# Ten held tiles instead of eight, a new block order and a first tile in four chunks in the quantized feed-forward of a gated Flamingo block

## The chip, the cores and the metric

The kernel runs on one core of one Trainium2 chip. The metric is device time in microseconds (us) for one execution of the whole kernel. The core has five engines with queues of their own: TensorE (PE, with its weight loads listed as PEld), VectorE (DVE), ScalarE (ACT), GpSimd (POOL) and SyncE (SP). Nearly all DMAs of this kernel are issued from SP's queue, which takes them strictly in the order in which they stand in it.

## The reference, cut to what matters

```
x = x + tanh(g_xattn) * cross_attention(layernorm(x), ctx)      # 4096 rows of 512
# feed-forward on n = layernorm(x), 512 -> 2048 -> 512
s_x = max|n| / 127 ;  xq = round(n / s_x)                       # one scale for the whole tensor
s_w = max|w| / 127 ;  wq = round(w / s_w)                       # the same for w1 and w2
h   = gelu((xq @ w1q.T + b1) * (s_w1 * s_x))                    # 4096 x 2048
s_h = max|h| / 127 ;  hq = round(h / s_h)                       # max over ALL of h
o   = (hq @ w2q.T + b2) * (s_w2 * s_h)
out = x + tanh(g_ffn) * o
```

The point that shapes the second half is `s_h`: the largest magnitude of all the middle activations `h` must be known before the first of them can be quantized. So no second-layer matmul can start until the whole first layer is done, and all 32 MB of `h` (float32) must be kept somewhere in the meantime.

## The kernel before, in words

The 4096 rows are cut into `NB` = 8 blocks of `TB` = 512 rows, and a block into `NT` = 4 row tiles of 128. Attention runs first (0 to about 440 us) and is not touched by the change; during it the weights are loaded and quantized into `w1q` (a tile of [128, 4, 2048] bf16, 16 KB per partition) and `w2q`. The rows of `x` stay in SBUF as `X[i]` throughout.

**First layer.** Its PE order is written out by hand (blocks 0 to 7, in each 16 feature chunks `fc`, in each 4 matmuls over `KC`). Block 0's quantized, transposed input is `xqT0`, made by PE transposes (L522 to L526). The inputs of the other blocks are made by `quantize_x(i+1)` on DVE: four normalizations of 512 columns (L169), one multiply-and-add-MAGIC over 2048 columns (L184), one subtract over 2048 columns (L185), and four DMA transposes from SP (L561) into `xqT`. The pool `fwork` has two buffers for `xs`, `xq` and `xqT`. Each group of four feature chunks forms one tile `G` ([128, 4, 512] float32, 8 KB per partition), written by four Gelu activations on ACT (L588), reduced for the maximum on DVE two chunks at a time (L598). A block has `GT` = 4 such tiles, so there are 32. The pool `gpool` has `HELD` = 8 buffers: the last 8 tiles (blocks 6 and 7) stay in SBUF in the dictionary `held`, the first 24 are stored to DRAM (L609, tensor `h`), 1 MB each, and come back later.

**The joint.** `scale_of(hmax, ...)` on DVE and PE turns the maxima into `s_h` and `inv_h` (L154 to L164). Then DVE computes `s2` = s_h * s_w2 * tanh(g_ffn) (L612, L613) and scales the bias row `b2_sb` by it (L614).

**Second layer.** Blocks are taken in the order 6, 7, 0, 1, 2, 3, 4, 5: the held ones first. Rounding a tile takes ACT (L634: times `inv_h`, plus MAGIC, in place) and then DVE (L635: minus MAGIC, into the bf16 tile `hq`). Tile 0 of block 6 is special: its first chunk is rounded on DVE alone (L631), its other three by ACT and DVE. The first block in the order runs feature chunks outside and row tiles inside, so that PE can begin with one chunk; every other block runs row tile by row tile, 16 matmuls each (L643), into the PSUM tile `pf` (pool `ps_o`, 4 buffers). Per row tile, POOL adds the bias row to `X` (L657), DVE adds the scaled PSUM result (L661), and SP stores 256 KB of output (L663). Loads of stored tiles, `Gb` (L628), go into `gpool` buffers as these come free. A scheduler places the loads between the output stores in SP's queue and the roundings between the L661 additions in DVE's queue; both queues keep their order at run time.

Of the kernel before, what the change touches and what calls it, by code (L numbers as in the profile page):

```python
# [8 lines left out]
F32 = mybir.dt.float32  # L9
BF16 = mybir.dt.bfloat16  # L10
AF = mybir.ActivationFunctionType
ALU = mybir.AluOpType
# [3 lines left out]
P = 128  # L16
D = 512
KC = D // P
# [9 lines left out]
TB = 512  # L28
NT = TB // P
FF = 2048  # L30
FC = FF // P
GF = 4
GT = FC // GF
HELD = 8
EPS = 1e-5
QP = 127.0
MIN_RANGE = 1e-6
MAGIC = 1.5 * 2.0**23
# [4 lines left out]
def tile_flamingo_gated_block(  # L43
# [20 lines left out]
    nc = tc.nc  # L64
    B = ctxT.shape[0]
    NB = x.shape[0] // TB
    NBB = NB // B

    const = ctx.enter_context(tc.tile_pool(name="const", bufs=1))
# [16 lines left out]
        return w.rearrange("(kc p) n -> p kc n", p=P)  # L86


    actx = ExitStack()
    awts = actx.enter_context(tc.tile_pool(name="awts", bufs=1))  # L90
    wq_sb = awts.tile([P, KC, D], F32, name="wq_sb")
    wo_sb = awts.tile([P, KC, D], F32, name="wo_sb")
# [7 lines left out]
    tg = const.tile([P, 2], F32, name="tg")  # L100
# [26 lines left out]
    mhalf = const.tile([P, NT], F32, name="mhalf")  # L127
    nc.gpsimd.memset(mhalf, -0.5)

    w1q = const.tile([P, KC, FF], BF16, name="w1q")  # L130
    xqT0 = const.tile([P, KC, TB], BF16, name="xqT0")
    w2q = const.tile([P, FC, D], BF16, name="w2q")
    mean2 = const.tile([P, NB, NT, 2], F32, name="mean2")
# [16 lines left out]
    def scale_of(maxima, name, psum, tag):  # L150


        m = const.tile([P, 1], F32, name=f"m_{name}")
        nc.vector.tensor_reduce(m, maxima, AX.X, ALU.max)  # L154
        diag = small.tile([P, P], F32, tag="diag", name=f"diag_{name}", bufs=1)
        nc.vector.tensor_scalar(diag, ident, m, None, ALU.mult)
        pg = psum.tile([P, 512], F32, tag=tag, name=f"pg_{name}")
        nc.tensor.matmul(pg[:, :P], ones, diag, start=True, stop=True)
        g = const.tile([P, 1], F32, name=f"g_{name}")
        nc.vector.tensor_reduce(g, pg[:, :P], AX.X, ALU.max)  # L160
        s = const.tile([P, 1], F32, name=f"s_{name}")
        nc.vector.tensor_scalar(s, g, MIN_RANGE, 1.0 / QP, ALU.max, ALU.mult)
        inv = const.tile([P, 1], F32, name=f"inv_{name}")
        nc.vector.reciprocal(inv, s)  # L164
        return s, inv

    def normalize2(dst, i, t):

        nc.vector.tensor_scalar(  # L169
            dst,  # L170
            X[i][:, t, :],
            mean2[:, i, t, 0:1],
            rstd2[:, i, t : t + 1],
            ALU.subtract,
            ALU.mult,
        )
# [5 lines left out]
    def quantize(dst, src, inv):  # L182

        nc.vector.tensor_scalar(src, src, inv, MAGIC, ALU.mult, ALU.add)  # L184
        return nc.vector.tensor_scalar(dst, src, MAGIC, None, ALU.subtract).ins  # L185
# [5 lines left out]
    with actx:  # L191
# [245 lines left out]
        for i in range(NB):  # L437
            for s in range(2 * NG):
                if s + 2 < 2 * NG:
                    last = softmax(i, s + 2)  # L440
                elif i + 1 < NB:
                    last = softmax(i + 1, s + 2 - 2 * NG)
# [47 lines left out]
                t = s - NT if i == 0 else s // 2  # L490
# [41 lines left out]
        tc.tile_pool(name="hidden_dram", bufs=1, space=bass.MemoryType.DRAM)  # L532
    )

    late = ctx.enter_context(tc.tile_pool(name="late", bufs=1, reuse_waits="tile"))
    b2_sb = late.tile([P, D], F32, name="b2_sb")
    nc.sync.dma_start(b2_sb, b2.to_broadcast([P, D]))

# [7 lines left out]
    with ExitStack() as fctx:  # L546
        fwork = fctx.enter_context(tc.tile_pool(name="fwork", bufs=2, reuse_waits="tile"))
        ps_h = fctx.enter_context(
            tc.tile_pool(name="ps_h", bufs=4, space=PSUM, reuse_waits="tile")
        )  # L550

        def quantize_x(i):

            xs = fwork.tile([P, NT, D], F32, tag="xs", name=f"xs{i}")
            xq = fwork.tile([P, NT, D], BF16, tag="xq", name=f"xq{i}")
            xqT = fwork.tile([P, KC, TB], BF16, tag="xqT", name=f"xqT{i}")
            for t in range(NT):
                normalize2(xs[:, t, :], i, t)
            quantize(xq, xs, inv_x)
            for t in range(NT):  # L560
                nc.sync.dma_start_transpose(xqT[:, :, t * P : (t + 1) * P], xq[:, t, :])  # L561
            return xqT

        s1 = const.tile([P, 1], F32, name="s1")
        nc.vector.tensor_tensor(s1, s_x, s_w1, ALU.mult)
        b1s = const.tile([P, FC], F32, name="b1s")
        nc.vector.tensor_scalar(b1s, b1_sb, s1, None, ALU.mult)
        fctx.enter_context(tc.manual_schedule(engines={mybir.EngineType.PE}))
        for i in range(NB):
            cur = xqT if i else xqT0  # L570
            if i + 1 < NB:
                with tc.issue_after(last):
                    xqT = quantize_x(i + 1)
            for a in range(GT):
                G = gtile(f"G{i}_{a}")
                for v in range(GF // 2):
                    for u in range(2):
                        fc = a * GF + 2 * v + u
                        ph = ps_h.tile([P, TB], F32, tag="ph", name=f"ph{i}_{fc}")
                        for kc in range(KC):  # L580
                            nc.tensor.matmul(  # L581
                                ph,
                                w1q[:, kc, fc * P : (fc + 1) * P],
                                cur[:, kc, :],
                                start=(kc == 0),
                                stop=(kc == KC - 1),
                            )
                        nc.scalar.activation(  # L588
                            G[:, 2 * v + u, :],
                            ph,  # L590
                            AF.Gelu,
                            bias=b1s[:, fc : fc + 1],
                            scale=s1,
                        )
                    k = (i * GT + a) * 2 + v
                    n = 1 if k == NB * GT * 2 - 1 else 2
                    for u in range(0, 2, n):
                        nc.vector.tensor_reduce(  # L598
                            hmax[:, k + u : k + u + 1],
                            G[:, 2 * v + u : 2 * v + u + n, :],  # L600
                            AX.XY,
                            ALU.max,
                            apply_absolute_value=True,
                        )
                if i * GT + a >= NB * GT - HELD:
                    held[i, a] = G
                else:
                    stored[i, a] = hidden_dram.tile([P, GF, TB], F32, name=f"h{i}_{a}")
                    nc.sync.dma_start(stored[i, a], G)  # L609
    s_h, inv_h = scale_of(hmax, "h", ps_g, "pg")  # L610
    s2 = const.tile([P, 1], F32, name="s2")
    nc.vector.tensor_tensor(s2, s_h, s_w2, ALU.mult)  # L612
    nc.vector.tensor_tensor(s2, s2, tg[:, 1:2], ALU.mult)  # L613
    nc.vector.tensor_scalar(b2_sb, b2_sb, s2, None, ALU.mult)  # L614

    hpool = ctx.enter_context(tc.tile_pool(name="hpool", bufs=2))
    ps_o = ctx.enter_context(tc.tile_pool(name="ps_o", bufs=NT, space=PSUM))
    first = NB - HELD // GT  # L620
    for i in [*range(first, NB), *range(first)]:
        hq = hpool.tile([P, FC, TB], BF16, tag="hq", name=f"hq{i}")
        for a in range(GT):
            if (i, a) in held:
                G = held[i, a]
            else:
                G = gtile(f"Gb{i}_{a}")
                nc.sync.dma_start(G, stored[i, a])  # L628
            done = 0
            if (i, a) == (first, 0):  # L630
                quantize(hq[:, 0, :], G[:, 0, :], inv_h)  # L631
                done = 1
            rest = G[:, done:, :]
            nc.scalar.activation(rest, rest, AF.Copy, bias=MAGIC, scale=inv_h)  # L634
            nc.vector.tensor_scalar(  # L635
                hq[:, a * GF + done : (a + 1) * GF, :], rest, MAGIC, None, ALU.subtract
            )
        po = {}

        def accumulate(t, fc):  # L640
            if fc == 0:
                po[t] = ps_o.tile([P, D], F32, tag="po", name=f"pf{i}_{t}")
            nc.tensor.matmul(  # L643
                po[t],
                hq[:, fc, t * P : (t + 1) * P],
                w2q[:, fc, :],
                start=(fc == 0),
                stop=(fc == FC - 1),
            )

        if i == first:
            for fc in range(FC):
                for t in range(NT):
                    accumulate(t, fc)
        for t in range(NT):
            y = X[i][:, t, :]
            nc.gpsimd.tensor_tensor(y, y, b2_sb, ALU.add)  # L657
            if i != first:
                for fc in range(FC):
                    accumulate(t, fc)  # L660
            nc.vector.scalar_tensor_tensor(y, po[t], s2, y, ALU.mult, ALU.add)  # L661
            r = i * TB + t * P
            nc.sync.dma_start(out[r : r + P, :], y)  # L663
# [62 lines left out]
```

## Time and profile before

| | before |
|---|---|
| median of 3 runs | 692.16 us (690.68 to 694.86) |
| the profiled execution | 692.1 us |
| its span in the trace | 690.0 us |
| attention and weights | 0 to about 442 us |
| scale of x, input of block 0 | 442 to 448.3 us |
| first layer (first to last `ph` matmul) | 448.3 to 560.3 us |
| scale of h | 560.3 to 563.6 us |
| second layer (first to last `pf` matmul) | 564.8 to 686.2 us |
| last addition and output store | 686.3 to 690.0 us |

The 2.1 us between span and time lie outside the trace. The page has six parts: busy time per engine, the span in 40 slices, DMA queues, the chain of work that ended last, groups of instructions, DMA issues. In a row of the groups stand line, engine, operation, output and inputs with their shapes, the count, the busy time in us, the mean in ns, and the idle time of the engine just before with what ended it. Long runs of one operation merge to one row in the timeline; a few per cent of matmul records are missing, so counts of matmuls there run low.

### The profile page before, as it was taken

Reading aid. Unit: us, or ns where it says so; the run is one execution under the profiler, and the core shown is the slowest. Engines: PE = TensorE matmul, PEld = TensorE weight load, DVE = VectorE, ACT = ScalarE, POOL = GpSimd, SP = SyncE. Lnnn points to the kernel's source line nnn. Section 1 sums busy time; section 2 is a strip of 40 time slices with the busy share of each in tenths; the row PEclk is TensorE's granted clock in tenths of the full one; section 3 lists DMA queues with packets and bytes.
Section 4 is the critical chain, followed back from the end, with each engine's and each line's share of the span. In section 5 each row is a group of like instructions: output and inputs, shape, how many; then the busy total and the mean of one; then the engine's idle time right before and its main releaser. Section 6 shows DMA issues by size and latency. Waiting matters only on the chain.

```text
span 690.0 us, 8178 instructions
## 1 busy us (share of the span) xinstructions
PE 651.0 (94%) x3027; PEld 324.3 (47%) x3048; DVE 518.4 (75%) x799; ACT 342.9 (50%) x472; POOL 200.7 (29%) x160
## 2 busy tenths in 40 slices
PE   4999999999999999999999999599999979999987
PEld 2655555455555455555455454244444424444433
DVE  3674686996996996975965757899998779865452
ACT  2455443344443344444344333179898979344540
POOL 2234323233233233233333332100000029991000
PEclk9999999999999999999999999799999989999999
DMA  9901100031131131100000000059999608798872
GB/s 299 353 2 58 65 1 0 1 119 65 62 123 61 62 117 66 62 0 1 1 0 1 1 16 1 0 153 353 318 312 358 183 9 345 262 347 321 315 275 76
DMA packets 41663, 89.09 MB, mean 129 GB/s; under 512 B 18763, under 2 KB 18763, under 8 KB 35480
## 3 DMA queue, kind: packets, MB, share of 16 engines
q1 hardware_dynamic: 39752, 87.21, 36.2%
q10 hardware_dynamic: 1872, 1.37, 0.7%
q8 instruction: 24, 0.39, 0.2%
q14 instruction: 15, 0.12, 0.1%
HBM read 51.34 MB, written 33.55 MB: 123 GB/s over the span
## 4 chain that ended last, share of the span: by engine, by line
PE 77%; DMA 8%; DVE 8%; ACT 4%; issue 2%; POOL 0%; SPq 0%; ACTq 0%; DVEq 0%
PE ph L581 16%; PE po L338 16%; PE pq L260 15%; PE pta L316 8%; DMA Gb<-h 7%; PE ps L279 6%; PE pf L643 6%; PE pc L325 6%; PE ptx L251 2%; ACT Gb L634 2%; DMA x<-in_x 1%; PE pvv L223 1%; PE pk L203 1%; DVE xf L169 1%; DVE tm L360 1%
## 5 line engine op out<-in xcount | busy, mean ns | idle before, releaser
L303 POOL TENSOR_TENSOR e<-e,rs 128x616 f32<-128x616 f32 x64 | 78.4, 1226 | 255.3 <-DVE rs L302 192.4
L643 PE MATMUL pf<-w2q,hq 128*128 128x512 bf16 x502 | 114.9, 388 | 8.4 <-DVE hq L635 4.6
L260 PE MATMUL pq<-xnT,wq_sb 128*128 128x512 f32 x256 | 117.9, 604 | 2.0 <-ACT xnT L252 2.0
L338 PE MATMUL po<-wo_sb,cT 128*128 128x512 f32 x256 | 117.6, 604 | 0.0
L581 PE MATMUL ph<-xqT,w1q 128*128 128x512 bf16 x501 | 111.3, 382 | 1.3 <-DVE xqT L526 0.5
L317 ACT COPY aT<-pta 77x512 f32<-77x512 f32 x128 | 72.4, 579 | 77.8 <-PE pta L316 77.7
L588 ACT ACTIVATE G<-ph,b1s,s 128x512 f32<-128x512 f32 x128 | 99.5, 777 | 14.0 <-PE ph L581 3.1
L657 POOL TENSOR_TENSOR x<-x,b_sb 128x512 f32<-128x512 f32 x32 | 57.8, 1848 | 125.2 <-DVE b_sb L614 125.2
L643 PEld LDWEIGHTS <-hq 128*128 128x128 bf16 x512 | 50.6, 100 | 72.4 <-issue 8.3
L598 DVE TENSOR_REDUCE hmax<-G 128x1 f32<-128x1024 f32 (+1 forms) x65 | 76.5, 1197 | 10.4 <-ACT G L588 10.3
L316 PE MATMUL pta<-ident,e 128*77 128x128 f32 x512 | 79.3, 280 | 1.7 <-ACT aT L317 1.2
L338 PEld LDWEIGHTS po<-wo_sb,cT 128*128 128x128 f32 x256 | 46.2, 189 | 71.7 <-issue 70.4
L581 PEld LDWEIGHTS <-w1q 128*128 128x128 bf16 x512 | 50.3, 99 | 62.0 <-issue 2.1
L316 PEld LDWEIGHTS pta<-ident,e 128*77 128x77 f32 x512 | 59.8, 147 | 40.6 <-issue 34.3
L298 ACT ACTIVATE e<-e 128x616 f32<-128x616 f32 x64 | 45.9, 717 | 60.2 <-DVE e L292 56.1
L288 DVE TENSOR_REDUCE mx<-ps 128x8 f32<-128x616 f32 x64 | 49.9, 780 | 30.3 <-PE ps L279 30.1
L260 PEld LDWEIGHTS pq<-xnT,wq_sb 128*128 128x128 f32 x256 | 46.8, 193 | 51.2 <-issue 47.2
L634 ACT ACTIVATE Gb<-Gb,inv_h 128x2048 f32<-128x2048 f32 x24 | 47.6, 1999 | 45.9 <-DMA Gb<-h 43.9
L300 DVE TENSOR_REDUCE sm<-e 128x8 f32<-128x616 f32 x64 | 50.4, 789 | 24.2 <-ACT e L298 23.9
L635 DVE TENSOR_SCALAR hq<-Gb 128x2048 bf16<-128x2048 f32 x24 | 38.2, 1600 | 30.5 <-ACT Gb L634 30.5
L292 DVE TENSOR_TENSOR e<-ps,mx 128x616 f32<-128x616 f32 x64 | 50.9, 796 | 2.9
L279 PE MATMUL ps<-kb,qT 64*128 64x154 f32 x512 | 52.7, 319 | 0.2
(89 smaller groups left out, 594.4 us busy)
## 6 DMA issues: line engine op xcount, KB each, us to landing
h<-G SPq DMA_DIRECT2D x24, 1024.0 KB, 6.2
Gb<-h SPq DMA_DIRECT2D x24, 1024.0 KB, 8.2
raw_w<-in_w2T SPq DMA_DIRECT2D x8, 1024.0 KB, 5.0
out_y<-x SPq DMA_DIRECT2D x32, 256.0 KB, 4.4
x<-in_x SPq DMA_DIRECT2D x7, 1024.0 KB, 5.4
raw_w<-in_w1T SPq DMA_DIRECT2D x4, 1024.0 KB, 11.7
x<-in_x SPq DMA_DIRECT2D x4, 256.0 KB, 3.5
wq_sb<-in_wqT ACTq DMA_DIRECT2D x1, 1024.0 KB, 9.6
```

The costliest lines, as they stand in the source:

```text
L260: nc.tensor.matmul(pq, wq_sb[:, kc, g * P : (g + 1) * P], xnT[i][:, kc, :], start=(kc == 0), stop=(kc == KC - 1),)
L279: nc.tensor.matmul(ps[:, q, u * RK : (u + 1) * RK], qT[i, g][r, t * P : (t + 1) * P], kblk[i // NBB][r, g, :], start=True, stop=True,)
L303: last["POOL"] = nc.gpsimd.tensor_tensor(e4, e4, rs[:, :, :, None].to_broadcast([P, 2, HG, NK]), ALU.mult).ins
L316: nc.tensor.transpose(pt[:NK, j, :], es[i, s][:, u, j, :], ident)
L317: nc.scalar.copy(aT[i, g][:, :, t * P : (t + 1) * P], pt[:NK, :, :])
L338: nc.tensor.matmul(po, cT[i, g][:, t * P : (t + 1) * P], wo_sb[:, g, :], start=(g == 0), stop=(g == NG - 1),)
L581: nc.tensor.matmul(ph, w1q[:, kc, fc * P : (fc + 1) * P], cur[:, kc, :], start=(kc == 0), stop=(kc == KC - 1),)
L588: nc.scalar.activation(G[:, 2 * v + u, :], ph, AF.Gelu, bias=b1s[:, fc : fc + 1], scale=s1,)
L598: nc.vector.tensor_reduce(hmax[:, k + u : k + u + 1], G[:, 2 * v + u : 2 * v + u + n, :], AX.XY, ALU.max, apply_absolute_value=True,)
L634: nc.scalar.activation(rest, rest, AF.Copy, bias=MAGIC, scale=inv_h)
L643: nc.tensor.matmul(po[t], hq[:, fc, t * P : (t + 1) * P], w2q[:, fc, :], start=(fc == 0), stop=(fc == FC - 1),)
L657: nc.gpsimd.tensor_tensor(y, y, b2_sb, ALU.add)
```

## The change

`HELD` goes from 8 to 10, so `gpool` gets ten buffers and tiles 2 and 3 of block 5 are held too; 22 tiles are stored and loaded instead of 24. To make room, `w1q` moves into a pool of its own, closed after the first layer; `xqT0` serves as transposed input for all even blocks, with one further `xqT` buffer for the odd ones; `quantize_x` works in two halves of two row tiles each, with half-size `xs` and `xq`.

In the second layer the block that is only partly held (5) comes after 6 and 7 and before 0 to 4. The first tile of block 6 is rounded wholly on DVE, in four chunks; `s2` is put behind these on DVE, and the scaling of `b2_sb` goes to POOL.

```diff
-HELD = 8
+HELD = 10
...
-    actx = ExitStack()
+    w1ctx, actx = ExitStack(), ExitStack()
+    w1q = w1ctx.enter_context(tc.tile_pool(name="w1q", bufs=1)).tile([P, KC, FF], BF16, name="w1q")
...
-    w1q = const.tile([P, KC, FF], BF16, name="w1q")
...
-    late = ctx.enter_context(tc.tile_pool(name="late", bufs=1, reuse_waits="tile"))
+    late = ctx.enter_context(tc.tile_pool(name="late", bufs=1, side="right", reuse_waits="tile"))
...
-            xs = fwork.tile([P, NT, D], F32, tag="xs", name=f"xs{i}")
-            xq = fwork.tile([P, NT, D], BF16, tag="xq", name=f"xq{i}")
-            xqT = fwork.tile([P, KC, TB], BF16, tag="xqT", name=f"xqT{i}")
-            for t in range(NT):
-                normalize2(xs[:, t, :], i, t)
-            quantize(xq, xs, inv_x)
-            for t in range(NT):
-                nc.sync.dma_start_transpose(xqT[:, :, t * P : (t + 1) * P], xq[:, t, :])
+            xqT = xqT0
+            if i % 2:
+                xqT = fwork.tile([P, KC, TB], BF16, tag="xqT", name=f"xqT{i}", bufs=1)
+            n = NT // 2
+            for t0 in range(0, NT, n):
+                xs = fwork.tile([P, n, D], F32, tag="xs", name=f"xs{i}_{t0}")
+                xq = fwork.tile([P, n, D], BF16, tag="xq", name=f"xq{i}_{t0}")
+                for t in range(n):
+                    normalize2(xs[:, t, :], i, t0 + t)
+                quantize(xq, xs, inv_x)
+                for t in range(n):
+                    r = slice((t0 + t) * P, (t0 + t + 1) * P)
+                    nc.sync.dma_start_transpose(xqT[:, :, r], xq[:, t, :])
...
+    w1ctx.close()
     s_h, inv_h = scale_of(hmax, "h", ps_g, "pg")
     s2 = const.tile([P, 1], F32, name="s2")
-    nc.vector.tensor_tensor(s2, s_h, s_w2, ALU.mult)
-    nc.vector.tensor_tensor(s2, s2, tg[:, 1:2], ALU.mult)
-    nc.vector.tensor_scalar(b2_sb, b2_sb, s2, None, ALU.mult)
...
-    hpool = ctx.enter_context(tc.tile_pool(name="hpool", bufs=2))
+    hpool = ctx.enter_context(tc.tile_pool(name="hpool", bufs=2, reuse_waits="tile"))
...
-    for i in [*range(first, NB), *range(first)]:
+    part = -(-HELD // GT) - HELD // GT
+    for i in [*range(first, NB), *range(first - part, first), *range(first - part)]:
...
-            done = 0
+            dst = hq[:, a * GF : (a + 1) * GF, :]
             if (i, a) == (first, 0):
-                quantize(hq[:, 0, :], G[:, 0, :], inv_h)
-                done = 1
-            rest = G[:, done:, :]
-            nc.scalar.activation(rest, rest, AF.Copy, bias=MAGIC, scale=inv_h)
-            nc.vector.tensor_scalar(
-                hq[:, a * GF + done : (a + 1) * GF, :], rest, MAGIC, None, ALU.subtract
-            )
+                for v in range(GF):
+                    last = quantize(dst[:, v, :], G[:, v, :], inv_h)
+
+                with tc.issue_after(last):
+                    nc.vector.tensor_tensor(s2, s_h, s_w2, ALU.mult)
+                    nc.vector.tensor_tensor(s2, s2, tg[:, 1:2], ALU.mult)
+                nc.gpsimd.tensor_scalar(b2_sb, b2_sb, s2, None, ALU.mult)
+            else:
+                nc.scalar.activation(G, G, AF.Copy, bias=MAGIC, scale=inv_h)
+                nc.vector.tensor_scalar(dst, G, MAGIC, None, ALU.subtract)
```

In the built program the order of instructions on PE is the same as before but for the block order. On DVE the first tile's operations stand as two multiplies, two subtracts, two multiplies, two subtracts, then the first `s2` product, the rounding of the second tile, and the second `s2` product. On SP the first five loads stand ahead of the first output store in both kernels; from there on one load follows nearly every output store.

## The prediction

> **What bounds the kernel now.** I read the page's busy shares and slices first, then the waits of the second layer alone, then the chain of waits in order of time.
>
> ```profile
> PE 651.0 (94%) x3027; PEld 324.3 (47%) x3048; DVE 518.4 (75%) x799; ACT 342.9 (50%) x472; POOL 200.7 (29%) x160
> ...
> PE   4999999999999999999999999599999979999987
> ...
> DMA  9901100031131131100000000059999608798872
> ```
>
> PE is busy nearly everywhere, so a gain can only come from its few dips: slices 1, 26, 33, 39 and 40 of 17.25 us. The last three lie at the joint and in the second layer. The waits from 560 us on (us in total, times, longest):
>
> ```profile
> ACT Gb L634 <- DMA Gb<-h: 43.9, 18, 7.9
> ...
> PE pf L643 <- DVE hq L635: 4.6, 4, 2.1
> ...
> PE pf L643 <- DVE x L661: 1.4, 1, 1.4
> ```
>
> PE waits little, but ACT waits 43.9 us for reloaded tiles: the reload is what runs late. The timeline's PE rows (start, us, and in brackets the idle time before) place PE's waits:
>
> ```profile
> 564.77 1.86 PE L643 MATMUL pf<-w2q,hq 128*128 128x512 bf16 x4 [1.80 <-issue]
> 567.29 14.72 PE L643 MATMUL pf<-w2q,hq 128*128 128x512 bf16 x59 [0.65 <-DVE hq L635]
> 583.45 71.82 PE L643 MATMUL pf<-w2q,hq 128*128 128x512 bf16 x325 [1.45 <-DVE x L661]
> 656.92 13.12 PE L643 MATMUL pf<-w2q,hq 128*128 128x512 bf16 x59 [1.65 <-DVE hq L635]
> 670.25 1.04 PE L643 MATMUL pf<-w2q,hq 128*128 128x512 bf16 x4 [0.21 <-DVE hq L635]
> 673.38 12.85 PE L643 MATMUL pf<-w2q,hq 128*128 128x512 bf16 x51 [2.09 <-DVE hq L635]
> ```
>
> From 583.45 PE has seven blocks left, 448 matmuls. At 0.216 us each (109.2 us for the last 505 of the first layer) that is 96.8 us; it takes 102.8, to 686.24. So **6.0 us** are lost late, and more at the start. What PE waits for late, the chain of waits shows:
>
> ```profile
> 650.03 7.26 DMA Gb<-h
> ...
> 657.37 2.01 ACT Gb L634
> ...
> 660.55 0.75 DVE x L661
> ...
> 661.32 0.33 SPq L663
> ...
> 661.75 8.23 DMA Gb<-h
> ```
>
> It is a ring: a load lands, ACT and DVE round it, only then does DVE reach the addition queued behind that rounding, only then does SP's queue reach the output store, and behind that store stands a later load. From 650.03 to 661.75 it turns in 11.7 us. By the order of SP's queue the loads at the two ends are Gb5_0 and Gb5_3, so a turn brings three tiles: 3.9 us a tile, where PE needs one per row tile of 16 x 0.216 = 3.46 us.
>
> **What the skill says.** The Trainium skill, "DMA: Bandwidth & Descriptors", section "Where 436 GB/s comes from", puts a core's HBM limit at about 358 GB/s. The trace agrees: 340 GB/s at a DMA share of 0.92 from 600 to 640 us; one load and one store a row tile, 1.31 MB per 3.46 us, would be 379. "SBUF — State Buffer", section "Who interferes with whom", says that a `tensor_scalar` in a two-port mode and a GpSimd operation block each other. The trace agrees: L635 takes 2276 ns on the seven whole held tiles, all beside POOL's L657, and 1.23 us from 626 us on, when POOL is done. "TensorE: Matmul & The Clock Gate", section "What's actually happening", gives about 3.4 us of activity before PE leaves half clock. Here matmuls stand 0.43 us apart after a pause, for 2.1 us at 449.09, 3.3 at 567.29 and 3.0 at 673.38.
>
> **The change, part by part.** The sum is made against the profiled 692.1 us (span 690.0 plus 2.1), as good as the median, 692.16.
>
> *Joint and first tile.* Before, from `inv_h` (L612 starts at 563.60) to the end of the first L661 (583.41) DVE works without a real pause, and this addition frees the PSUM buffer that PE waits 1.45 us for: DVE sets this stage. After, by DVE's new queue: four multiplies (start to start 0.40 us at L184) and four subtracts (0.34 at L185) take 2.96, to 566.56; the first `s2` product 0.12, to 566.68. The second tile, ready from ACT at 563.66 + 2.0 = 565.7, takes 1.15 without POOL beside it, to 567.8; the second product, to 567.95. Only now can POOL begin, with the moved bias scaling (1787 ns, row L455 on the same shape; DVE's L614 of 480 ns goes away), so L657 starts at about 569.8 instead of 565.14. The third tile, ready from ACT at 567.7, ends at 569.1; the remaining five run against POOL, 17.35 us for eight L635 less 1.84 leaves 2.22 each: from 569.7 to 580.8. The first L661 ends at 581.5, **1.9 us earlier**. If bias scaling already blocks the third tile, 0.8 earlier. PE itself: its first chunk stands two operations deeper (hq at 564.83 against 564.67, +0.15), then it has no 0.65 us gap, and ends block 6 at 564.9 + 3.3 (7.7 matmuls at half clock) + 56.3 x 0.216 = 580.4, ahead of DVE. ACT loses one operation (1577 ns).
>
> *Two held tiles more.* Two stores and two loads of 1 MB go. In SP's queue a load now stands two row tiles earlier against PE's need: the last, Gb4_3, is behind the third output of the block that is sixth in order; before, Gb5_3 was behind the first of the seventh. That is 6.9 us of lead. The ring also gets longer: Gb2_2 leads to hq2_2, the first addition of block 1, its store, Gb3_2, so four tiles per turn. Does DMA keep up? From 567.26 to 670.01 it brought 24 loads and 25 stores of 0.26 MB, 31.7 MB, 309 GB/s. At that mean rate 22 loads and 23 stores (29.1 MB) take 94.3 us and end at about 661; rounding (3.2) and the 52 matmuls left behind the last tile (11.2) give 675.7. PE alone from 581.5 gives 678.3. So PE is later than the loads, and all **6.0 us** go. From the other side: if DMA can't serve four tiles a turn faster than three, it stays at 3.9 us a tile; over 19 row tiles the lag is 8.5 us against a lead of 7.5 (19.9 us from the third output of the sixth block to the need, less 12.4 for landing and rounding), 1 to 3 us stay lost. I take 6.0; the end for the range is 3.
>
> *Order 6, 7, 5, 0 to 4.* No cost: the two loads for block 5 are in the first five, in flight at 567 to 577 as before, and needed at 595.
>
> *First layer.* Quantizing in halves gives 14 DVE operations more. From 1.19 to 0.40 us (L184) and 1.13 to 0.34 (L185) over 2048 and 512 columns follow 0.66 and 0.60 for 1024, so 0.2 us per block, 1.4 in all. DVE idles 0.51 us per pair of chunks from 528 us on, 18 times, 9 us: hidden. A new wait: half-size `xq` has two buffers, so a half needs the transposes of the same half one block before landed, and DVE's reductions (L598) queue behind it. By queue order this holds DVE 2 to 3 us in blocks 2 and 3 and keeps it in step with the transposes from then on; its last half is rounded at about 532, and 21 reductions of 1.13 us bring it to 556, before ACT's last Gelu at 559.4. Nobody else waits for those reductions, as buffers are now ten deep. Three normalizations stand ahead of the copy that completes `xqT0` (L526), with only 0.4 and 0.7 us of idle to hide in: +0.2 us, on the path. SP: the first transpose of a block is now ahead of the last store, and may start when PE leaves the buffer, at a block's start instead of 1.5 us after. As DMA is full here (share 0.94 to 1.09 per block), I cost this at nothing. Bounds: the last transpose of a block landed 0.6 to 1.4 us before PE needed it, so it can gain nothing, but lose. Attention: only addresses move; 0, no row prices it.
>
> Sum: -1.9 + 0.2 - 6.0 = -7.7, so 692.1 - 7.7 = **684.4 us**.
>
> **The rivals.** *A, the ring still binds at the end* (DMA is at its limit, and more loads in flight land later; 8 us instead of 5 speaks for it). 3 us of the 6 stay: 687.4. *B, the first layer pays* (slower). The transposes into `xqT0` and the one odd buffer stand in the same full DMA queues, and the halves wait for each other. If the last one lands later by d, each of six blocks starts late by d minus about 1.0 us of margin, and nothing hides it. With d above 2.3 us (1.3 x 6 = 7.7) the whole gain is gone, with d = 3 it is 12, 696.4 us. Against it: the same bytes, started earlier. *C, no net effect*: the ring's saving is real but half a microsecond to a microsecond per block goes as in B, or the clock drops at other pauses: 690 to 692.
>
> **How the numbers follow.** Half a per cent, 3.46 us, is about what a measurement of this kernel can tell from no change: faster means below 688.7, slower above 695.6. Forecast 0.62 (682.3 to 686.3), A 0.18, C 0.10, B 0.10. Faster is the forecast plus A, 0.80; same 0.10; slower 0.10. The range runs from 682.0 (block 6's handover at PE's own 580.4, and the spread between runs) to 689.5, which takes in A and touches C.
>
> **What would show it.** Right: `pf` from about 564.9 without the gap before the second chunk, PE resuming at 581.6, then no wait for hq above 0.5 us, last matmul near 678.5; ACT's wait for Gb well under 43.9 us; first layer still ending near 560.5. Wrong: idle PE at block starts in the first layer with `xqT` as releaser (B), or waits for hq in the last two blocks (A).

## The result, and the profile after

| | before | after |
|---|---|---|
| median of the runs made together | 691.42 us (690.5 to 694.86, 4 runs) | 684.38 us (683.54 to 684.96, 4 runs) |
| the profiled execution, its span | 692.1, 690.0 us | 683.97, 682.2 us |
| `inv_h` ready (start of its reciprocal) | 563.52 | 563.05 |
| PE resumes after the first L661/L668 | 583.45 | 581.40 |
| start of the last PSUM addition | 686.34 | 678.36 |

The ratio is 0.9879 (95% interval 0.9852 to 0.9907): faster by 1.2%. Ratios, here and below, are estimated over all runs but two slow ones of the kernel before, which took 857 and 2315 us, and are not the quotient of two medians (0.9898 here). Lines have moved: the roundings L634 and L635 are now L643 and L644, the matmul L643 is L650, POOL's addition L657 is L664, DVE's addition L661 is L668, the store L663 is L670.

Busy times, and the slices' rows of PE and of its granted clock, now of 17.06 us each:

```profile
PE 648.7 (95%) x3027; PEld 324.3 (48%) x3048; DVE 519.2 (76%) x817; ACT 341.4 (50%) x471; POOL 202.2 (30%) x161
...
PE   4999999999999999999999999689999988999997
...
...
PEclk9999999999999999999999999979999997999999
```

The joint is still there (slices 33 and 34, with a lowered clock in 34, from 562.8 us on). The dip in slice 39 is gone; the 7 in slice 40 is the end itself, after PE's last matmul. PE's rows in the timeline show it exactly:

```profile
564.53 16.62 PE L650 MATMUL pf<-w2q,hq 128*128 128x512 bf16 x63 [2.02 <-DVE hq L185]
581.40 96.85 PE L650 MATMUL pf<-w2q,hq 128*128 128x512 bf16 x439 [0.25 <-DVE x L668]
```

There is no pause after the first chunk, and from 581.40 on one unbroken row of 96.85 us to the end. Where before three waits for `hq` stood in the last 35 us, none is left. The waits from 560 us on:

```profile
ACT Gb L643 <- DMA Gb<-h: 38.0, 17, 5.3
DVE x L668 <- PE pf L650: 26.2, 11, 2.7
```

DVE now waits for PE's results. ACT still waits 38.0 us for loads, which costs nothing, since PE waits for none of them.

The span fell by 7.8 us. From `inv_h` to PE's resumption it went from 19.93 to 18.35 (-1.58), from there to the last addition from 102.89 to 96.96 (-5.93). The attention phase, whose operations the change leaves as they were, ended 0.43 earlier in this execution. The rest is +0.14: -0.04 between attention and `inv_h`, +0.18 behind the last addition.

### The profile page after: what moved, and what is told of

Its sections match the earlier page's. It is cut to its first block, busy times and chain, and to the rows that moved or that the text cites. A ratio compares the mean times of both kernels' runs of the same rounds, so it can differ in the third digit from the quotient of the medians.

```text
span 682.2 us, 8191 instructions
## 1 busy us (share of the span) xinstructions
PE 648.7 (95%) x3027; PEld 324.3 (48%) x3048; DVE 519.2 (76%) x817; ACT 341.4 (50%) x471; POOL 202.2 (30%) x161
## 4 chain that ended last, share of the span: by engine, by line
PE 88%; DVE 7%; ACT 2%; DMA 1%; issue 1%; POOL 0%; SPq 0%; ACTq 0%; DVEq 0%
PE pf L650 16%; PE ph L586 16%; PE po L338 16%; PE pq L260 15%; PE pta L316 8%; PE ps L279 6%; PE pc L325 6%; PE ptx L251 2%; DMA x<-in_x 1%; PE pvv L223 1%; PE pk L203 1%; DVE xf L169 1%; DVE tm L360 1%; ACT aT L317 1%; DVE sm L300 1%
## 5 line engine op out<-in xcount | busy, mean ns | idle before, releaser
L650 PE MATMUL pf<-w2q,hq 128*128 128x512 bf16 x502 | 112.9, 385 | 2.8 <-DVE hq L185 2.0
L593 ACT ACTIVATE G<-ph,b1s,s 128x512 f32<-128x512 f32 x128 | 99.6, 778 | 13.8 <-PE ph L586 3.1
L650 PEld LDWEIGHTS <-hq 128*128 128x128 bf16 x512 | 50.7, 99 | 64.8 <-issue 3.5
L643 ACT ACTIVATE Gb<-Gb,inv_h 128x2048 f32<-128x2048 f32 x22 | 43.7, 2002 | 38.0 <-DMA Gb<-h 38.0
L664 POOL TENSOR_TENSOR x<-x,b_sb 128x512 f32<-128x512 f32 x32 | 56.2, 1795 | 0.1
L268 ACT ACTIVATE qT<-pq,bq_sb 128x512 f32<-128x512 f32 x32 | 22.0, 687 | 55.3 <-PE pq L260 55.3
```

Of the source, the lines that this page charges most:

```text
L593: nc.scalar.activation(G[:, 2 * v + u, :], ph, AF.Gelu, bias=b1s[:, fc : fc + 1], scale=s1,)
L650: nc.tensor.matmul(po[t], hq[:, fc, t * P : (t + 1) * P], w2q[:, fc, :], start=(fc == 0), stop=(fc == FC - 1),)
```

## The experiments

The start of `inv_x`, just after attention, lay between 443.3 and 445.7 us over the profiles. That spread is there by 25 us (the second group of `pq` matmuls starts between 22.5 and 24.9 us), and the runs e1 to e12 have the changed kernel's attention, so it does not come from their edits. From `inv_x` to `inv_h` it was 119.6 to 120.4 us. The table counts from `inv_h`. "Handover" is from there until PE resumes with the second block, "PE's last part" from that to the start of the last PSUM addition; 96.96 is this part without a wait. Ratios are to the kernel before, measured beside each run on the same chip.

| kernel | handover | PE's last part | median (range, runs) | ratio |
|---|---|---|---|---|
| before | 19.93 | 102.89 | | |
| after | 18.35 | 96.96 | 684.38 (683.54-684.96, 4) | 0.9879 |
| e1_held8 | 18.56 | 99.80 | 689.82 (687.75-692.13, 7) | 0.9942 |
| e2_oldjoint | 19.94 | 96.96 | 688.0 (687.58-688.49, 5) | 0.991 |
| e3_held8_oldjoint | 19.95 | 105.99 | 694.7 (691.15-696.61, 14) | 1.0008 |
| e4_held8_bufs10 | 18.59 | 96.97 | 685.29 (684.22-685.95, 4) | 0.9869 |
| e5_order_last | 18.63 | 101.26 | 687.79 (684.53-693.71, 18) | 0.9943 |
| e6_held9 | 18.29 | 96.96 | 685.33 (683.85-686.4, 6) | 0.9902 |
| e8_warm | 17.59 | 98.62 | 684.93 (682.86-686.99, 6) | 0.9897 |
| e9_warm_latepool | 16.05 | 96.96 | 683.8 (682.09-684.27, 5) | 0.9876 |
| e10_latepool | 18.45 | 96.96 | 685.7 (685.25-687.94, 6) | 0.9902 |
| e11_after_again | 18.34 | 96.96 | 685.43 (684.47-686.38, 6) | 0.9894 |
| e12_warm_latepool_again | 16.05 | 96.96 | 683.39 (682.48-683.84, 5) | 0.9862 |

The edits are given against the changed kernel.

### The two parts apart: e1, e2, e3

e1 takes back the held tiles alone:

```diff
-HELD = 10
+HELD = 8
```

> The changed kernel with HELD back at 8 (ten buffers become eight, order 6, 7, 0 to 5, 24 stores and loads), the new first tile kept. Theory (the two parts add up; the late 6.0 us belong to the held tiles): 684.4 + 6 = 690.4, down to 689.8 if it is before less the 1.6 us that the joint measured; PE waits for hq again in the last two blocks. Rival 1 (the joint is the gain, the loads were hidden anyway): 684.4. Rival 2 (the ring of loads ends last and does not start earlier when PE does, so the joint's gain is eaten): 691.4, as before.

e2 takes back the first tile and the place of `s2` and the bias scaling alone:

```diff
+    nc.vector.tensor_tensor(s2, s_h, s_w2, ALU.mult)
+    nc.vector.tensor_tensor(s2, s2, tg[:, 1:2], ALU.mult)
+    nc.vector.tensor_scalar(b2_sb, b2_sb, s2, None, ALU.mult)
...
+            done = 0
             if (i, a) == (first, 0):
-                for v in range(GF):
-                    last = quantize(dst[:, v, :], G[:, v, :], inv_h)
...
+                quantize(hq[:, 0, :], G[:, 0, :], inv_h)
+                done = 1
```

> The changed kernel with ten held tiles but the joint as it was before (one chunk on VectorE, three through ScalarE, s2 and the bias scaling ahead on VectorE). Theory: the loads have slack, so the joint's time lies bare: 684.4 + 1.6 = 686.0, PE resuming about 19.9 us after inv_h, and no wait for hq in the last blocks. Rival (with ten tiles the end is set elsewhere and the joint is hidden): 684.4.

e3 makes both edits, so that of the change only the halves in the first layer, the use of `xqT0`, and the places and settings of the pools are left:

> The changed kernel with HELD = 8 and the old joint: what is left of the change is the first layer in halves, xqT0 used again, and the placing of the pools. Theory: costs 0 to 0.2 us, so 691.4 to 691.6, equal to before. Rival (the halves or the placing gain or cost by themselves): outside 690.4 to 692.6.

PE's rows of e3 from the handover on:

```profile
583.51 58.00 PE L650 MATMUL pf<-w2q,hq 128*128 128x512 bf16 x263 [1.52 <-DVE x L668]
642.26 14.20 PE L650 MATMUL pf<-w2q,hq 128*128 128x512 bf16 x62 [0.75 <-DVE hq L642]
658.50 15.67 PE L650 MATMUL pf<-w2q,hq 128*128 128x512 bf16 x63 [2.04 <-DVE hq L642]
676.35 13.04 PE L650 MATMUL pf<-w2q,hq 128*128 128x512 bf16 x51 [2.17 <-DVE hq L642]
```

Those of e2:

```profile
569.72 14.88 PE L650 MATMUL pf<-w2q,hq 128*128 128x512 bf16 x59 [0.67 <-DVE hq L642]
585.90 96.85 PE L650 MATMUL pf<-w2q,hq 128*128 128x512 bf16 x439 [1.30 <-DVE x L668]
```

And those of e1:

```profile
584.36 71.82 PE L650 MATMUL pf<-w2q,hq 128*128 128x512 bf16 x325 [0.25 <-DVE x L668]
657.21 13.99 PE L650 MATMUL pf<-w2q,hq 128*128 128x512 bf16 x63 [1.04 <-DVE hq L644]
672.66 11.40 PE L650 MATMUL pf<-w2q,hq 128*128 128x512 bf16 x51 [1.46 <-DVE hq L644]
```

e3 behaves like the kernel before (1.0008, interval 0.9988 to 1.0027): handover 19.95, and waits for `hq` at the ends of blocks. So the rest of the change costs and brings nothing that shows within about 0.3%. In absolute time e3 missed its band of 690.4 to 692.6, but the kernel before, measured beside it, also stood higher, at 693.8 us (median of 18). The ratios are what counts here.

e2 has the old handover and no late wait. e1 has the new handover and late waits. So the new first tile shortens the handover, by 1.4 us without the held tiles (19.95 to 18.56) and by 1.6 with them (19.94 to 18.35), and the held tiles take away the late loss.

How large that loss is varies. With eight buffers it was 5.9 us in the profile of before, 9.0 in e3 and 2.8 in e1, while it was 0.0 in each profile of e2, e4 and after. Not all of it is waiting. In e3 two of the pauses, of 2.04 and 2.17 us, were followed by PE at half clock: the 64 matmuls of the row at 658.50 (63 recorded) took 15.67 us where 64 x 0.216 is 13.8, and the 52 of the last row (51 recorded) 13.04 where it is 11.2. By that estimate 3.7 of the 9.0 us are half clock.

The two parts do not simply add. e1's median lies 4.9 us below that of e3, measured together, and the handover explains only 1.4. So on average the new first tile also shortened the late loss, by about 3 us. This e1's expectation had not foreseen: it set e1 at most 1.6 us below the kernel before, and by the ratio it came out about 4.0 below. Why an earlier handover, or the different order on DVE, shortens the late loss stays open.

### Less traffic, or more buffers: e4, e5, e6

Two held tiles do two things. They take 2 MB of stores and 2 MB of loads away, and they give the pool ten buffers, so that loads are issued earlier before PE needs them (their lead). e4 keeps 24 stored tiles and gives them ten buffers:

```diff
-HELD = 10
+HELD = 8
...
-    gpool = ctx.enter_context(tc.tile_pool(name="gpool", bufs=HELD, side="right", reuse_waits="tile"))
+    gpool = ctx.enter_context(tc.tile_pool(name="gpool", bufs=10, side="right", reuse_waits="tile"))
```

> The changed kernel with 8 tiles held and 24 stored and loaded, but the pool of G tiles still with ten buffers, so two loads can start before the joint. Separates fewer bytes from more buffers. Theory (what counts is the lead of the loads over PE, two buffers): 684.4 to 685.4, no wait for hq in the last blocks. Rival (the two loads and two stores saved are what counts, DMA being at its limit): 689 to 690.4.

e5 does the reverse. It has 22 stored tiles, but takes the partly held block last, so that two buffers stay occupied until the end and eight turn:

```diff
-    for i in [*range(first, NB), *range(first - part, first), *range(first - part)]:
+    for i in [*range(first, NB), *range(first)]:
```

> The changed kernel, ten tiles held, but the blocks in the order 6, 7, 0, 1, 2, 3, 4, 5, so the two held tiles of block 5 sit in their buffers to the end and only eight turn over; 22 loads as in the changed kernel. Separates the two loads saved from the two buffers more in the ring. Theory (lead of the loads): the ring is that of eight buffers until the sixth and seventh block, so PE waits for hq again in the block before the last; the last block has two of its tiles on chip and waits less. 2 to 4 us slower than the changed kernel, and a wider spread of times. Rival (bytes alone): as the changed kernel.

e6 holds nine:

```diff
-HELD = 10
+HELD = 9
```

> The changed kernel with nine held tiles (one of block 5), 23 stores and loads, nine buffers. Theory: one row tile, 3.46 us, of lead instead of two; the late loss with eight was 2.8 us in the trace of the new joint with eight held (HELD = 8), and up to 9 us in that with the old joint, so one tile takes away most but not all of it: 0 to 2 us slower than the changed kernel, and a spread between that of eight and of ten. Rival (all or nothing, the ring's turn of four tiles needs ten): 4 to 5 us slower, as with eight.

e4's one PE row from the handover to the end:

```profile
583.38 96.85 PE L650 MATMUL pf<-w2q,hq 128*128 128x512 bf16 x439 [0.25 <-DVE x L668]
```

e5's rows:

```profile
584.14 58.00 PE L650 MATMUL pf<-w2q,hq 128*128 128x512 bf16 x268 [0.25 <-DVE x L668]
642.94 13.12 PE L650 MATMUL pf<-w2q,hq 128*128 128x512 bf16 x60 [0.80 <-DVE hq L644]
656.97 1.04 PE L650 MATMUL pf<-w2q,hq 128*128 128x512 bf16 x4 [0.91 <-DVE hq L644]
660.08 25.21 PE L650 MATMUL pf<-w2q,hq 128*128 128x512 bf16 x116 [2.08 <-DVE hq L644]
```

e4 moves every byte that before moved and loses nothing (0.9869, interval 0.9843 to 0.9894). But it does not move them at the same time. Two of its 24 loads are issued before the joint, from 543.8 us on, a stretch in which DMA is nearly idle in after (share 0.01 from 540 to 556); e4's issues from 500 to 566 us show them (count, size, median us to landing):

```profile
h<-G SPq DMA_DIRECT2D x12, 1024.0 KB, 5.9
Gb<-h SPq DMA_DIRECT2D x2, 1024.0 KB, 5.9
```

After 566 us e4 therefore has 22 loads and 31.54 MB, exactly as the changed kernel, against 24 and 33.64 MB in before. e4 shows that the 4 MB need not be saved over the whole kernel. It does not show that ten buffers would be enough with 24 loads left for the second layer; no run tried that.

e5 is the other half. It too has 22 loads and 31.54 MB after 566 us, but only eight turning buffers, and it waits again. Its profiled execution took 691.05 us, in the slower part of its wide range (684.53 to 693.71); by all its runs the ratio is 0.9943 (0.9921 to 0.9966), the same as that of e1 with eight buffers and all the bytes (0.9942). **So less traffic alone does not take the late loss away; the lead that ten turning buffers give is needed.** By the same token the block order 6, 7, 5 counts for something: it turns the two held tiles back into buffers early.

How much lead is left can be read off. PE needs the last tile of the last block 11.2 us (52 matmuls) before its end, at 667.1 in after, and DVE's last rounding ends at 663.3. These margins were 3.8 us in after, 5.9 in e11, 8.3 in e2, 6.3 in e4, and 2.0 in e6 with nine tiles. With eight there is none: PE resumes 0.06 us after that rounding in the profile of before. Nine were enough in the run profiled, with little to spare.

### What sets the handover: e8, e9, e10, e11, e12

In the joint of the changed kernel, DVE's and POOL's rows (x<-x,b_sb is POOL's L664) read:

```profile
567.46 1.22 DVE L644 TENSOR_SCALAR hq<-G 128x2048 bf16<-128x2048 f32 x1
567.70 3.12 POOL L641 TENSOR_SCALAR b_sb<-b_sb,s 128x512 f32<-128x512 f32 x1 [128.17 <-issue]
569.13 1.23 DVE L644 TENSOR_SCALAR hq<-G 128x2048 bf16<-128x2048 f32 x1 [0.46 <-ACT G L643]
569.98 10.89 PEld L650 LDWEIGHTS <-hq 128*128 128x128 bf16 x51 [0.21 <-issue]
570.91 14.84 POOL L664 TENSOR_TENSOR x<-x,b_sb 128x512 f32<-128x512 f32 x8
571.03 8.89 DVE L644 TENSOR_SCALAR hq<-G 128x2048 bf16<-128x2048 f32 x4 [0.67 <-ACT G L643]
580.59 2.73 DVE L668 SCALAR_TENSOR_TENSOR x<-pf,s,x 128x512 f32<-128x512 f32 x4 [0.68 <-issue]
```

DVE is done with its roundings at 579.92 and then idle for 0.68 us before its first addition. It is PE that comes last: its weight loads stood 0.43 us apart until 569.98, twice the 0.216 us of a matmul at full clock, so PE ran at half clock for 5.45 us from 564.53. The two candidates are thus half clock on PE and roundings of 2.22 us beside POOL on DVE. e8 removes the first. It keeps PE busy with 16 matmuls whose result nobody reads, written into PE's order before and after the scale of `h`:

```diff
+    def keep_busy(n):
+        pw = ps_w.tile([P, D], F32, tag="pw", name="pw")
+        for _ in range(n):
+            nc.tensor.matmul(pw, w2q[:, 0, :P], w2q[:, 1, :], start=True, stop=True)
...
+        keep_busy(8)
...
+    with tc.manual_schedule(engines={mybir.EngineType.PE}):
+        s_h, inv_h = scale_of(hmax, "h", ps_g, "pg")
+        keep_busy(8)
```

> The changed kernel with PE kept busy over the joint: eight matmuls on w2q into a PSUM tile that nobody reads before the maximum's matmul, eight behind it. In the changed kernel PE ran at half clock for 5.45 us from 564.53 on, which costs 2.7 us of block 6. Theory: PE is what ended block 6 there, by 0.68 us over VectorE; with a full clock PE ends block 6 at 578.4 but VectorE's roundings end at 579.9 as before, so the gain is 0.7 us, from inv_h to the last addition 114.6 us instead of 115.3. Rival (PE alone sets the handover): 2.7 us, 112.6 us.

PE's rows of e8, and its table by stretches (columns: stretch; its length; busy time of PE, PEld, DVE, ACT, POOL; granted clock; DMA share; GB/s):

```profile
566.29 13.99 PE L660 MATMUL pf<-w2q,hq 128*128 128x512 bf16 x64 [0.30 <-DVE hq L185]
582.41 98.51 PE L660 MATMUL pf<-w2q,hq 128*128 128x512 bf16 x448 [2.13 <-DVE x L678]
```

```profile
582.00:586.00 4.00, 3.59 (x9) 1.24 (x9) 4.00 (x5) 4.00 (x4) 4.00 (x4) 0.57 0.78 298
```

The first block takes PE 13.99 us instead of 16.62, but now PE waits 2.13 us for DVE, and after that pause its clock falls to half for a while (0.57 from 582 to 586). PE's last part is 1.7 us longer, and the gain of 0.8 at the handover is lost. The last addition came 116.2 us after `inv_h`, where 114.6 was expected; the expectation had the handover right and did not foresee the second half-clock stretch. e9 holds POOL back as well: the held blocks are rounded up front, `s2` and the bias scaling follow, and in the first block POOL adds the bias after DVE's addition:

```diff
+    for i in blocks[:2]:
+        early[i], last = rounded(i)
+    with tc.issue_after(last):
+        nc.vector.tensor_tensor(s2, s_h, s_w2, ALU.mult)
+        nc.vector.tensor_tensor(s2, s2, tg[:, 1:2], ALU.mult)
+    nc.gpsimd.tensor_scalar(b2_sb, b2_sb, s2, None, ALU.mult)
...
+            if i == first:
+                nc.gpsimd.tensor_tensor(y, y, b2_sb, ALU.add)
```

> As the last, and GpSimd is held back: the products for s2 stand behind the last held tile's rounding, so bias scaling and the bias additions begin only then, and block 6 gets its bias after its PSUM addition. VectorE's roundings then run at 1.23 us instead of 2.22 and are paced by ScalarE's 1.9 us a tile, ending at about 577.9. Theory (shared port is what slows VectorE in the joint): from inv_h to the last addition 112.6 us, 2.7 us less than the changed kernel. Rival (VectorE is slowed by something else, or the bias additions come back later on the path): 114 to 116 us.

e10 is e9 without the 16 matmuls, e11 the changed kernel and e12 e9 again, these three on one chip:

> Held blocks rounded up front, POOL's bias scaling and the bias additions of the first block behind them; PE is not kept busy over the joint. Theory 1 (DVE's roundings beside POOL set the handover alone): as with PE kept busy, PE resumes 16.05 us after inv_h and the last addition comes at about 113.0. Theory 2 (PE's half clock after its pause is the second limit, close behind): PE ends the first block of the second layer about 2.7 us later than at full clock, at 17.0 to 17.9 us after inv_h, resumes with a wait of under 0.7 us on DVE, and the last addition comes at 114.3 to 115.1: a gain of 0.2 to 1.0 us over the changed kernel.

> The changed kernel as it is, to stand beside the two others on the same chip. From the start of the reciprocal that gives inv_h to the last PSUM addition its profile showed 115.3 us; expected again within 0.3 us, with PE's last part 97.0 us and no wait of PE for hq above 0.5 us after the second block's first addition. Median time about 0.988 of the kernel before.

> The version with PE kept busy and POOL held back, once more, on one chip with the changed kernel. If the 2.3 us that its trace gained between inv_h and the last addition are real, they are there again (113.0 +- 0.3) and the median time is 0.9966 of the changed kernel's (684.4 to 682.1). If PE's shorter way only moves the half-clock window to another pause, the last addition comes later than 114.5 after inv_h in this profile.

The handover in e10 (DVE's row):

```profile
581.89 2.73 DVE L677 SCALAR_TENSOR_TENSOR x<-pf,s,x 128x512 f32<-128x512 f32 x4 [2.51 <-PE pf L659]
```

The same in e12:

```profile
566.66 13.99 PE L669 MATMUL pf<-w2q,hq 128*128 128x512 bf16 x64 [0.30 <-DVE hq L185]
578.83 1.23 DVE L651 TENSOR_SCALAR hq<-G 128x2048 bf16<-128x2048 f32 x1 [0.67 <-ACT G L650]
580.48 1.57 POOL L661 TENSOR_SCALAR b_sb<-b_sb,s 128x512 f32<-128x512 f32 x1 [139.42 <-PE pf L669]
581.23 2.97 PE L669 MATMUL pf<-w2q,hq 128*128 128x512 bf16 x13 [0.59 <-DVE x L687]
```

With POOL out of the way alone (e10) DVE waits 2.51 us for PE, and the first addition comes 17.65 us after `inv_h`, against 17.54 in after: no gain, and less than even the second theory expected. With PE kept busy alone it comes at 16.80, with both at 15.24. Two limits lie 0.7 us apart, and only taking both away brings the 2.3 us. The last addition comes 113.0 us after `inv_h` in e9 and in e12, against 115.3 in after and e11 and 115.4 in e10; for e9 112.6 had been expected. On one chip the medians of e12 and e11 are 683.39 and 685.43 us (0.997 of each other, without an interval; the two ranges do not touch), and e10's is 685.7. **Measured beside both kernels, e12 is the fastest**, at 0.9862 of before (0.9837 to 0.9887). The margin over the changed kernel is about 0.3%; it rests on this one comparison and on the two traces, since e9's ratio, 0.9876 on another chip, cannot be told from the 0.9879 of after. What paces the first addition of e12 is ACT, at 1.91 us a tile, for which DVE waits 0.67 us each time. PE is close behind again: by its row (580.65 less three matmuls) the first result is ready at about 580.0, and the addition starts at 580.42.

## Why the prediction was right

The forecast was 684.4 us; the median came out at 684.38. That the figures are so close is partly luck, since errors of about a microsecond cancelled or were swallowed by the spread. The span fell by 7.8 us where 7.7 was forecast, but 0.43 of it came from the attention phase, which the forecast put at nothing.

*The ring at the end (-6.0).* Right in mechanism and size for the profiled execution: 5.93 us went. The argument through the lead was the right one, as e4 and e5 show: PE, not DMA, is later at the end. Rival A's 3 us did not stay. The other argument, the mean rate of 309 GB/s, is weaker than it looks. The loads ended near the estimated 661 (ACT begins its last tile at 660.04), but in e11, the same kernel, that tile began 2.1 us earlier after `inv_h`. Nor does the 340 GB/s that the prediction set beside a limit of about 358 show a limit there: in after the loads alone moved 423 GB/s from 570 to 580 us. What the prediction did not see is that 6.0 us was one draw from a loss of 2.8 to 9.0. The change takes away the spread too: the six runs of the changed kernel in e11 lie within 1.9 us, the eleven of the kernel before beside them within 7.2 (688.67 to 695.86).

*The joint (-1.9).* The size was nearly right (-1.58), the reason in part wrong. The failed step is "PE ... ends block 6 at 580.4, ahead of DVE", which took 3.3 us of half clock; it was 5.45, so PE ended 18.1 us after `inv_h` instead of the 16.9 worked out. The trace of before could have told it: its first four matmuls, at 564.77, took 1.86 us, so half clock began there and not at 567.29, and lasted until 570.6, 5.9 us. PE came after DVE, which had finished its roundings 0.4 us earlier than worked out. Against that, the bias scaling on POOL was taken at 1787 ns and took 3.12 us. This delayed POOL's own additions, so that four roundings instead of five ran beside them at 2.22 us: a mis-sized term that turned out in favour.

*First layer (+0.2, otherwise nothing).* From `inv_x` to the last copy into `xqT0` 4.03 us became 4.17, so +0.14. From `inv_x` to `inv_h` it was 119.77 before and 119.73 after, so none of it arrived there; and with 119.6 to 120.4 over all profiles, a cost of 0.2 cannot be told from none. The new wait of DVE for the transposes, taken at 2 to 3 us, came to 1.0 us, once. Rival B, the only one that ended slower, did not come about: from 448 us to the end of the first layer PE waited for an `xqT` only once, for 0.7 us before block 0 (L526), and e3 shows the first layer's edits free within 0.3%. Rival C has nothing for it either.

*Markers.* `pf` from 564.53 without a gap, PE resuming at 581.40, the last matmul at 678.26 and no wait for `hq` were as listed. "ACT's wait for Gb well under 43.9" was a poor marker: it was still 38.0, and 32.2 in e4 against 44.4 in e1, which says little about the end. What counts is whether PE waits.

## What to carry to other kernels

When loads go through a ring of buffers and share an in-order queue with stores that wait for the results, count the lead of the last load against the consumer's need before counting bytes: with less traffic and eight turning buffers (e5) the late loss stayed here, and with ten (e4, after) it was gone. A stage with two engines that end within a microsecond of each other gives little for speeding up either: here 0.8 us at the handover for PE, lost again later (e8), and nothing for DVE (e10). Take the time of the second limit first, then remove both. And where a loss depends on such a race, one profile shows one draw of it, so look at the spread of the times too.

## What the runs showed of the hardware that was not expected

- The half clock after the joint's pause lasted 5.45 us, not about 3.4. The Trainium skill, "TensorE: Matmul & The Clock Gate", section "What's actually happening", describes a free-running window of about 3.4 us, which allows for more than one window's length after the first matmul; the prediction had used one. The same section has the clock fall only after an idle window of about 3.4 us. Here a pause of 2.13 us was enough (e8, clock 0.57 after it), and so were 2.04 and 2.17 us in e3. Yet after 2.08 us in e5 PE kept its clock (116 matmuls in 25.21 us, 0.217 each), as it did after 1.45 us in the kernel before at 583.45 (clock 1.00 from 581 to 600). So near 2 us the length of the pause alone did not decide. A window that runs on regardless of the pause would fit this, and in e3 the clock fell only when PE was working again (0.87 from 658.5 to 659.5 us, 0.50 from 659.5 to 662.5); no run tests it.
- DVE and POOL did not share the delay evenly. "SBUF — State Buffer", section "Who interferes with whom", says that whoever comes first blocks the other wholly. In after, two roundings of 1.22 and 1.23 us kept their pace while POOL's bias scaling stretched to 3.12 us (1.57 in e12, with no rounding beside it). Against POOL's eight additions in a row it was DVE that went from 1.23 to 2.22 us, while an addition took 1.86 us, against 1.27 in e12 with no rounding beside it. That the two slow each other agrees with the page. That the second rounding kept its pace although the bias scaling had started before it does not follow from order alone, and these runs do not show what decides.
